# Row sums of the softmax: from a column of ones in the products to ScalarE's accumulator

## The chip, the cores and the metric

The kernel runs on one core of a Trainium2 chip. The metric is the device time of one execution in microseconds; the median of three runs before the change is 420.76 us (420.61 to 422.99). Everything is float32. The engines are TensorE (PE; its weight loads are PEld), VectorE (DVE), ScalarE (ACT), GpSimd (POOL) and SyncE (SP), which issues most DMAs. Each works through its own queue in order and waits on semaphores for the others.

## The reference

Cross-attention with a second, small set of image-prompt tokens. B = 8 batches, S = 112 queries, 20 heads of D = 16, 371 text tokens and NIP = 4 prompt tokens a batch:

```python
q = heads(hidden_states @ W_q)
k_t = heads(text_ehs @ W_k)
v_t = heads(text_ehs @ W_v)
probs_t = softmax(einsum('bhsd,bhtd->bhst', q, k_t) * attn_scale)
text_out = einsum('bhst,bhtd->bhsd', probs_t, v_t)
qsem = l2norm(einsum('bhst,bte->bhse', probs_t, text_ehs))
ip_n = l2norm(ip_ehs)
sem = einsum('bhse,bne->bhsn', qsem, ip_n)
fused = einsum('bhsd,bhnd->bhsn', q, k_ip) * attn_scale + 0.5 * sem
probs_ip = softmax(fused) * spatial_mask[None, None, :, None]
out = (text_out + einsum('bhsn,bhnd->bhsd', probs_ip, v_ip)) @ W_out + b_out + residual
```

The softmax over the 371 tokens divides by the row sum of its exponentials. The kernel keeps the exponentials undivided, multiplies them with everything that they meet, and divides once at the end; it therefore needs the row sum z of each query and head.

## The kernel before, in words

The work goes through 40 **steps**: for each of 8 batches b, five groups g of four heads (`steps`, line 1121). The four heads of a group sit on the four 32-row groups of TensorE and work side by side.

For one step, in the order of the data:

- `scores` (line 724) multiplies queries and keys of one head into a PSUM bank: 371 text columns and 4 prompt columns. The keys of all heads stand in `kT`, three pieces of T = 375 columns, one piece for every two groups.
- `probabilities` (line 753): VectorE takes the negated maximum of the row (line 757), ScalarE writes the exponentials to `p` (line 760) and copies the four prompt logits to `ipl` (line 762). `sent` (line 766) lets SP issue the DMA that carries `p` to the ring buffer `xg` in blocks of 28 queries, so that
- `turned` (line 771) can transpose them in 32x32 blocks on VectorE to `xgT`.
- `multiplied` (line 784) is the large product. Its stationary operand is a block of 32 tokens of the transposed exponentials of one head; its moving operand is a row of `u`. One head has 12 blocks. `u` holds, side by side, the Gram matrix of the batch's context (upper part only, so block j begins at column 32j), the products with the four normalised prompts, a column of ones, and the 16 values of the head. A product is therefore up to UW = 371 + 4 + 1 + 16 = 392 columns wide and ends 32 columns earlier with every block, 40 at the last one. A float32 product is two TensorE instructions in the trace.
- `value_sums` (line 807, ScalarE) copies the last 21 columns of the result to `pvs`: four prompt products, the row sum z (from the column of ones), and 16 value sums. `reduced` (line 839, VectorE) multiplies the first 371 columns with `p` again and sums them: that is the squared norm of `qsem`. In the last batch and at the end of the one before it, `shared` (line 812) does this for some heads on ScalarE and GpSimd, and ScalarE then sums with an accumulator output (line 836).
- `finish` (line 860) turns `pvs` and the norms of a whole batch into its output; z is read in lines 881 to 898. It runs in pieces, spread over the next batch. For the last batch it is split: 16 heads in `finish`, four in `last_heads` (line 1045).

`u` is built a batch ahead. The Gram matrix goes through PSUM to `ug` (ScalarE, line 512), whose constant columns are set once (lines 220 to 223), and from there by DMA into the four row groups of `u` (`gram_to_groups`, line 554). The values are put into the last 16 columns of each region by GpSimd (`placed`, line 696). The regions of a row begin at `GCOL` = 0, 392, 656, and a row quarter is `GW` = 792 columns.

The order on TensorE, SP, VectorE and, in the main loop, ScalarE is the order of the program text (`manual_schedule`); GpSimd is ordered by the framework until the last batch. The scores and exponentials run LEAD = 2 steps ahead of the products (`ahead`, line 1257): in step n, two scores of step n+2 are issued before the first block and two more after block j = 5, and in between the transposes for step n+1. After the blocks come `value_sums`, `reduced`, and then `between` (line 1132): one piece of the work for the next batch on TensorE (its Gram matrix, values, keys, queries) or of the output of the batch before. `pvs` and `u` have two buffers, used by the batches in turn; the products use four PSUM banks (`ps_qd`), each free again when both `value_sums` and `reduced` have read it.

Of the kernel before, what the change touches and what calls it, by code (L numbers as in the profile page):

```python
# [8 lines left out]
F32 = mybir.dt.float32  # L9
AF = mybir.ActivationFunctionType  # L10
ALU = mybir.AluOpType
# [3 lines left out]
NIP = 4  # L15
# [5 lines left out]
def kernel(  # L21
# [14 lines left out]
    nc = tc.nc  # L36
    P = 128
    B, S, C = x.shape
    T, E = ehs.shape[1:]
    H = HEADS  # L40
    D = C // H
    TT = T - NIP
# [7 lines left out]
    REST = C - FULL * P  # L50
    RG = 32
    HN = H * NIP
    VW = NIP + 1 + D
    UW = TT + VW
    UV = UW - D
    SCALE = D ** -0.5
# [8 lines left out]
    GCOL = [sum(WC[:c]) for c in range(NT + 1)]  # L65
# [7 lines left out]
    groups = [[i * HC + 2 * a + r for a in range(GROUP)] for i in range(2) for r in range(2)]  # L73
# [4 lines left out]
    work = ctx.enter_context(tc.tile_pool(name="work", bufs=2))  # L78
# [140 lines left out]

    ug = const.tile([P, GCOL[NT]], F32, tag="ug", name="ug")  # L220
    for c in range(NT):
        nc.gpsimd.memset(ug[:, GCOL[c + 1] - D - 1 : GCOL[c + 1] - D], 1.0)
        nc.gpsimd.memset(ug[:, GCOL[c + 1] - D : GCOL[c + 1]], 0.0)


# [178 lines left out]
    def begin(b):  # L404
        s = st[b] = dict(ct=loaded.pop(b))
        s["ctxT"] = work.tile([P, NE, TP], F32, tag="ctxT", name=f"ctxT_{b}")
        if b < LEAD:
            nc.gpsimd.memset(s["ctxT"][:, :, T:], 0.0)

        s["kT"] = work.tile([P, NC, T], F32, tag="kT", name=f"kT_{b}")  # L410
        s["k3"] = k3
        if b == 0:
            s["vd"] = dram.tile([TP, C], F32, tag="vd", name=f"vd_{b}", bufs=1)
        s["u"] = work.tile([P, UCOL], F32, tag="u", name=f"u_{b}")
        s["vr"] = work.tile([P, BLK, NG, D], F32, tag="vr", name=f"vr_{b}")
        s["ipl"] = work.tile([S, H, NIP], F32, tag="ipl", name=f"ipl_{b}")
        s["ss"] = work.tile([S, H], F32, tag="ss", name=f"ss_{b}")
        s["pvs"] = work.tile([S, H, VW], F32, tag="pvs", name=f"pvs_{b}")

    def dealt(b, c, t):  # L420

# [321 lines left out]
    def home(b, g):  # L743

        if b == B - 1 and g == 1:
            t = io.tile([P, NT, E], F32, tag="ct", name=f"p_{b}_{g}").rearrange("p c e -> p (c e)")
        elif b == B - 1 and g == 3:
            t = wv_sb.rearrange("p e f -> p (e f)")
        else:
            return work.tile([S, GROUP, TT], F32, tag="p", name=f"p_{b}_{g}", bufs=3)  # L750
        return t[:S, : GROUP * TT].rearrange("p (a t) -> p a t", t=TT)

    def probabilities(b, g, a, hold=False):
        s = st[b]
        ps = s.pop(("sc", g, a))
        nmx = small.tile([S, 1], F32, tag="nmx", name=f"nmx_{b}_{g}_{a}", bufs=4)
        nc.vector.tensor_reduce(nmx, ps[:S, :TT], AX.X, ALU.max, negate=True)  # L757
        if ("p", g) not in s:
            s["p", g] = home(b, g)
        nc.scalar.activation(s["p", g][:, a, :], ps[:S, :TT], AF.Exp, bias=nmx)  # L760
        if b > 0:
            nc.scalar.copy(s["ipl"][:, groups[g][a], :], ps[:S, TT:T])  # L762
        if not hold:
            sent(b, g, a)

    def sent(b, g, a):

        xg = x_ring[(b * NG + g) % NX]
        nc.sync.dma_start(xg[a * RG : a * RG + S // QN, :, :TT], st[b]["p", g][:, a, :])
# [37 lines left out]
    def value_sums(b, g, a0=0, a1=GROUP):  # L807
        s = st[b]
        for h, ps in list(zip(groups[g], s["qd", g]))[a0:a1]:
            nc.scalar.copy(s["pvs"][:, h, :], ps[:S, TT:UW])  # L810

    def shared(b, g, n):

        s = st[b]
        some = list(enumerate(zip(groups[g], s["qd", g])))[:n]
        if b == B - 1:
            t = work.tile([P, NE, TP], F32, tag="ctxT", name=f"shared_{b}_{g}")
            prods = [t[:S, a, :TT] for a, _ in some]
        else:

            t = work.tile([S, NIP, H, D], F32, tag="wv", name=f"shared_{b}_{g}", bufs=1)
            t = t.rearrange("p n h d -> p (n h d)")
            prods = [t[:, a * TP : a * TP + TT] for a, _ in some]
        p = s["p", g]
        for a, (h, ps) in some:
            if b == B - 1:
                nc.scalar.copy(s["pvs"][:, h, :], ps[:S, TT:UW])
            nc.scalar.copy(prods[a], ps[:S, :TT])
        yield

        for a, _ in some:
            nc.gpsimd.tensor_tensor(prods[a], prods[a], p[:, a, :], ALU.mult)
        yield

        for a, (h, _) in some:
            nc.scalar.activation(prods[a], prods[a], AF.Copy, accum_out=s["ss"][:, h : h + 1])
        yield
# [22 lines left out]
    def finish(b, heads=(0, H), bd=None):  # L860

        s = st[b]
        eng = nc.gpsimd
        h0, h1 = heads
        n = h1 - h0
# [11 lines left out]
        pvs = s["pvs"][:, part]  # L877
        if "xb" not in s:
            s["xb"] = work.tile([S, C], F32, tag="xb", name=f"xb_{b}", bufs=1)
            with_bias(b)  # L880
        z = pvs[:, :, NIP]

        z2 = sm("z2")
        nc.vector.scalar_tensor_tensor(z2, z, EPS * EPS, z, ALU.mult, ALU.mult)
# [2 lines left out]
        zr = sm("zr")  # L887
        attn = attn_ring[b % 2]
        ah = attn[:, :C].rearrange("p (h d) -> p h d", d=D)[:, part]

        def divided():
            eng.tensor_tensor(
                ah, pvs[:, :, NIP + 1 :], zr.unsqueeze(2).to_broadcast([S, n, D]), ALU.mult
            )

        if bd is not None:
# [33 lines left out]
        if bd is not None:  # L930
            ps = bank(f"ps_wT_{b}")
# [9 lines left out]
            ps = bank(f"ps_a_{b}_{h0}")  # L941
# [103 lines left out]
    def last_heads(b):  # L1045


        s = st[b]
        h0, n = FULL * HC, GROUP
        part = slice(h0, H)  # L1050

        def sm(name, *shape):
            return small.tile([S, n, *shape], F32, tag=f"{name}l", name=f"{name}_last", bufs=1)

        def over_ip(t):
            return t.unsqueeze(2).to_broadcast([S, n, NIP])

        pvs = s["pvs"][:, part]
        z = pvs[:, :, NIP]
        z2, rn, zr = sm("z2"), sm("rn"), sm("zr")  # L1060
        nc.vector.scalar_tensor_tensor(z2, z, EPS * EPS, z, ALU.mult, ALU.mult)
        yield

        nc.vector.tensor_tensor(rn, s["ss"][:, part], z2, ALU.max)
        nc.vector.reciprocal(zr, z)
        attn = attn_ring[b % 2]
        nc.vector.tensor_tensor(
            attn[:, :C].rearrange("p (h d) -> p h d", d=D)[:, part],
            pvs[:, :, NIP + 1 :],
            zr.unsqueeze(2).to_broadcast([S, n, D]),  # L1070
            ALU.mult,
        )
        nc.scalar.activation(rn, rn, AF.Sqrt)
        nc.scalar.preload_act_table(AF.Exp)
        ps = ps_qd.tile([P, 512], F32, tag="qd", name=f"ps_a_{b}_{h0}")
        nc.tensor.transpose(ps[:, :S], attn[:, FULL * P :], ident[:S, :S])
        yield

        nc.vector.reciprocal(rn, rn)
        fu, ex, w = sm("fu", NIP), sm("ex", NIP), sm("w", NIP)  # L1080
        nc.vector.tensor_tensor(fu, pvs[:, :, :NIP], over_ip(rn), ALU.mult)
        nc.vector.scalar_tensor_tensor(fu, fu, SEM_SCALE, s["ipl"][:, part], ALU.mult, ALU.add)
        mx, sx, rx = sm("mx"), sm("sx"), sm("rx")
        nc.vector.tensor_reduce(mx, fu, AX.X, ALU.max)
        nc.vector.tensor_tensor(fu, fu, over_ip(mx), ALU.subtract)
        nc.scalar.activation(ex, fu, AF.Exp)
        yield

        aT = work.tile([P, NC, S], F32, tag="aT", name=f"aT_{b}_{h0}")
        nc.scalar.copy(aT[:, FULL, :], ps[:, :S])  # L1090
        nc.vector.tensor_reduce(sx, ex, AX.X, ALU.add)
        nc.vector.reciprocal(rx, sx)
        nc.vector.scalar_tensor_tensor(w, ex, sm_sb, over_ip(rx), ALU.mult, ALU.mult)
        yield

        k = n * NIP
        ps = ps_qd.tile([P, 512], F32, tag="qd", name=f"ps_wT_{b}_{h0}")
        nc.tensor.transpose(ps[:k, :S], w.rearrange("s h n -> s (h n)"), ident[:S, :S])
        wT = small.tile([S, S], F32, tag="wTl", name="wT_last", bufs=1)
        nc.scalar.copy(wT[:k], ps[:k, :S])  # L1100
        yield

        nc.tensor.matmul(
            s["o"][:S, :C], aT[:, FULL, :], wo_sb[:, FULL, :], start=False, stop=False
        )
        nc.tensor.matmul(s["o"][:S, :C], wT[:k], s["bw"], start=False, stop=True)
        yield

        ob = work.tile([S, C], F32, tag="xb", name=f"ob_{b}", bufs=1)
        nc.vector.tensor_tensor(ob, s["o"][:S, :C], s["xb"], ALU.add)  # L1110
        nc.sync.dma_start(out[b], ob)
        del st[b]
        yield
# [247 lines left out]
    b = B - 1  # L1361
# [6 lines left out]
    for g in range(NG):  # L1368
# [7 lines left out]
        for j, _ in enumerate(multiplied(b, g)):  # L1376
# [8 lines left out]
            if g == 1 and j in (2, 3):  # L1385
                for a in ((3, 2), (1, 0))[j - 2]:
                    ps = ps_qd.tile([P, 512], F32, tag="qd", name=f"ps_s_{b}_{NG - 1}_{a}")
# [9 lines left out]
        n = (3, 3, 2, 1)[g]  # L1397
# [93 lines left out]
```

## Time and profile before

| | before |
|---|---|
| median of 3 runs | 420.76 us |
| the profiled execution's own time | 420.08 us |
| its span, first to last instruction | 418.3 us |
| TensorE busy | 410.9 us, 98% |
| VectorE busy | 334.5 us, 80% |
| ScalarE busy | 216.3 us, 52% |
| GpSimd busy | 123.6 us, 30% |
| the products of line 797, busy on TensorE | 218.5 us, 3840 instructions |
| the exponentials of line 760, busy on ScalarE | 84.5 us, 156 instructions, and 4 that write elsewhere |

A row of a group of instructions reads: line, engine, operation, output<-inputs by name, shape of output<-input, count, then busy time in us and the mean of one in ns, then idle time of the engine just before them and what ended it. A row of the timeline reads: start in us, length in us, engine, line, operation, names, shapes, count. A row of the chain reads: start, length, what. A row of the waits: who waited for whom, us in total, times, the longest. PE's matmuls overlap in the pipeline and the ends of their records are modelled, so starts say more than lengths. A wait for several semaphores is put down to the one that came last.

### The profile page before, as it was taken

The numbers are of one execution on the slowest core, as the hardware profiler recorded it, in microseconds if no ns is written. First come the engines' busy times: TensorE is split into PE (matmuls) and PEld (weight loads), VectorE is DVE, ScalarE is ACT, GpSimd is POOL, SyncE is SP. The second block draws the span as 40 slices with busy tenths as digits, with TensorE's granted clock in tenths as the row PEclk, the third lists the DMA queues.
The fourth block names the chain that finished last, engine by engine and source line by source line (L and its number), as shares of the span: only waits on it lengthen the run. The fifth ranks groups of instructions, "written<-read, shape, count | busy, mean of one in ns | idle before, by whom it ended". The sixth has DMA issues, their size and how long they took to land.

```text
span 418.3 us, 14151 instructions
## 1 busy us (share of the span) xinstructions
PE 410.9 (98%) x5512; PEld 321.4 (77%) x5512; DVE 334.5 (80%) x724; ACT 216.3 (52%) x732; POOL 123.6 (30%) x308
## 2 busy tenths in 40 slices
PE   8999999999999999999999999999999999989996
PEld 8767777787778877788777877788678887677983
DVE  4037689988899889898898978899798977878774
ACT  2344334736365453746356353654538463765774
POOL 3611121112071114422062121712144120724540
PEclk9999999999999999999999999999999999999999
DMA  8777856557764455465554555554445355526201
GB/s 247 211 189 201 184 144 155 150 133 172 176 164 130 134 142 142 113 157 164 142 134 126 170 133 136 133 126 143 121 123 137 97 169 151 144 75 168 69 2 31
DMA packets 47578, 58.98 MB, mean 141 GB/s; under 512 B 10648, under 2 KB 41536, under 8 KB 47510
## 3 DMA queue, kind: packets, MB, share of 16 engines
q1 hardware_dynamic: 46878, 57.10, 51.8%
q10 hardware_dynamic: 632, 0.96, 0.8%
q8 instruction: 44, 0.72, 0.8%
q14 instruction: 24, 0.20, 0.2%
HBM read 16.79 MB, written 1.88 MB: 45 GB/s over the span
## 4 chain that ended last, share of the span: by engine, by line
PE 90%; DVE 3%; POOL 2%; ACT 2%; DMA 2%; issue 1%; SPq 0%; DVEq 0%; POOLq 0%
PE ps_qd L797 37%; PE ps_v L616 13%; PE ps_s L734 10%; PE ps_k L582 10%; PE ps_g L540 7%; PE ps_q L381 3%; PE ps_o L1011 3%; PE ps_g L496 1%; DMA xg<-p 1%; DVE nmx L757 1%; ACT p L760 1%; DVE xgT L778 1%; PE ps_w L472 1%; PE ps_o L966 1%; PE ps_k L598 1%; POOL wv L986 1%
## 5 line engine op out<-in xcount | busy, mean ns | idle before, releaser
L797 PE MATMUL ps_qd<-u,xgT 32*112 32x168 f32 (+11 forms) x3840 | 218.5, 351 | 0.0
L797 PEld LDWEIGHTS ps_qd<-u,xgT 32*112 32x112 f32 x3840 | 185.0, 172 | 27.2 <-issue 0.7
L778 DVE STREAM_TRANSPOSE xgT<-xg 128x512 f32<-128x512 f32 (+2 forms) x79 | 126.0, 1604 | 4.3 <-DMA xg<-p 3.9
L760 ACT ACTIVATE p<-ps_s,nmx 112x371 f32<-112x371 f32 x156 | 84.5, 579 | 86.5 <-DVE nmx L757 81.2
L757 DVE TENSOR_REDUCE nmx<-ps_s 112x1 f32<-112x371 f32 x160 | 78.4, 534 | 25.1 <-PE ps_s L734 24.1
L843 DVE CUSTOM_DVE_ANT_0 junk<-ps_qd,p 112x371 f32<-112x371 f32 x146 | 79.2, 543 | 20.3 <-ACT pvs L810 3.3
L703 POOL COPY u<-vr 128x64 f32<-128x64 f32 x120 | 26.7, 240 | 138.4 <-PE ps_qd L797 106.5
L734 PE MATMUL ps_s<-kT,qm 32*112 32x375 f32 (+1 forms) x320 | 65.8, 496 | 0.0
L616 PE MATMUL ps_v<-wv_sb,ctxT 128*128 128x384 f32 (+1 forms) x192 | 63.0, 477 | 0.0
L616 PEld LDWEIGHTS ps_v<-wv_sb,ctxT 128*128 128x128 f32 x192 | 35.7, 190 | 20.9
L582 PE MATMUL ps_k<-ctxT,wk_sb 128*128 128x371 f32 x136 | 46.9, 488 | 0.2 <-DVE ctxT L463 0.2
L734 PEld LDWEIGHTS ps_s<-kT,qm 32*112 32x112 f32 x320 | 25.6, 171 | 12.7 <-issue 10.8
L582 PEld LDWEIGHTS ps_k<-ctxT,wk_sb 128*128 128x128 f32 x136 | 24.4, 189 | 14.0 <-issue 0.5
L651 ACT COPY vr<-vext 32x240 f32<-32x240 f32 x84 | 32.7, 389 | 1.3
L623 ACT COPY vext<-ps_v 128x384 f32<-128x384 f32 (+1 forms) x24 | 11.2, 466 | 42.2 <-PE ps_v L616 42.2
L540 PE MATMUL ps_g<-ctxT 128*32 128x375 f32 (+11 forms) x672 | 30.4, 333 | 0.0
L540 PEld LDWEIGHTS ps_g<-ctxT 128*32 128x32 f32 x672 | 27.7, 110 | 2.0
L390 DVE TENSOR_SCALAR qm<-ps_q,emask 128x224 f32<-128x224 f32 (+1 forms) x25 | 9.0, 394 | 18.1 <-PE ps_q L381 18.0
L762 ACT COPY ipl<-ps_s 112x4 f32<-112x4 f32 x140 | 23.0, 165 | 0.0
L986 POOL TENSOR_TENSOR wv<-vip,w 112x1280 f32<-112x1280 f32 x6 | 14.8, 2468 | 22.2 <-DVE w L926 22.2
L512 ACT ACTIVATE ug<-ps_g 128x375 f32<-128x375 f32 (+2 forms) x24 | 8.3, 375 | 24.7 <-PE ps_g L540 12.5
L442 DVE STREAM_TRANSPOSE ctxT<-ct 128x512 f32<-128x512 f32 x18 | 20.0, 1113 | 0.0
(177 smaller groups left out, 344.2 us busy)
## 6 DMA issues: line engine op xcount, KB each, us to landing
xg<-p SPq DMA_DIRECT2D x156, 162.3 KB
u<-ug SPq DMA_DIRECT2D x124, 99.0 KB
ct<-in_ctx_dram SPq DMA_DIRECT2D x24, 176.0 KB
vip<-vipd SPq DMA_DIRECT2D x6, 560.0 KB
out_dram<-ob SPq DMA_DIRECT2D x8, 140.0 KB
ct<-in_ctx_dram SPq DMA_DIRECT2D x4, 256.0 KB
x_sb<-in_x_dram SPq DMA_DIRECT2D x7, 140.0 KB
xr_sb<-in_x_dram SPq DMA_DIRECT2D x28, 35.0 KB
```

The costliest lines, as they stand in the source:

```text
L540: nc.tensor.matmul(ps[c][q * RG : (q + 1) * RG, j * RG - c * P : T - c * P], ctxT[:, e, j * RG : (j + 1) * RG], ctxT[:, e, j * RG : T], st ...
L582: nc.tensor.matmul(ps[:, :TT], wk_sb[:, e, i * P : (i + 1) * P], s["ctxT"][:, e, :TT], start=(e == 0), stop=(e == NE - 1),)
L616: nc.tensor.matmul(ps[:, :w], ctxT[:, e, c * P : (c + 1) * P], wv_sb[:, e, :w], start=(e == 0), stop=(e == NE - 1),)
L651: copy(s["vr"][a * RG : (a + 1) * RG, q::QN].rearrange("p c g d -> p c (g d)"), s["vext"][q * RG : (q + 1) * RG, :, a * w : (a + 1) * w],)
L703: nc.gpsimd.tensor_copy(v, dealt(b, c, s["vr"][:, c * QN : (c + 1) * QN, g, :]))
L734: nc.tensor.matmul(ps[:S, :w], qm[a * RG : (a + 1) * RG, i, r, j * S : (j + 1) * S], s["kT"][a * RG : (a + 1) * RG, i, :w], start=True, st ...
L757: nc.vector.tensor_reduce(nmx, ps[:S, :TT], AX.X, ALU.max, negate=True)
L760: nc.scalar.activation(s["p", g][:, a, :], ps[:S, :TT], AF.Exp, bias=nmx)
L762: nc.scalar.copy(s["ipl"][:, groups[g][a], :], ps[:S, TT:T])
L778: nc.vector.transpose(xT[:, j0:j1].rearrange("p j (k q) -> p q j k", q=QN), xg[:, :, j0 * RG : j1 * RG].rearrange("p q (j k) -> p q j k", ...
L797: nc.tensor.matmul(banks[a][:S, j * RG : UW], xT[a * RG : (a + 1) * RG, j, :S], region(b, c)[a * RG : (a + 1) * RG, q, j * RG - c * P :], ...
L843: nc.vector.tensor_tensor_reduce(out=junk, in0=ps[:S, :TT], in1=s["p", g][:, a, :], scale=1.0, scalar=0.0, op0=ALU.mult, op1=ALU.add, accu ...
```

## The change

The column of ones leaves `u`. The exponential's ACTIVATE gets an accumulator output instead, which writes the row sum of what it has just computed to the last column of `pvs`. `pvs` keeps its width of 21: four prompt products, 16 value sums, and the row sum at the end. The products are one column narrower (391 to 39), `GCOL` becomes 0, 391, 654 and `GW` 789, and the copies of `value_sums` have 20 columns. The place of z in `finish` and `last_heads` moves accordingly.

```diff
-    VW = NIP + 1 + D
+    VW = NIP + D
     UW = TT + VW
     UV = UW - D
...
     for c in range(NT):
-        nc.gpsimd.memset(ug[:, GCOL[c + 1] - D - 1 : GCOL[c + 1] - D], 1.0)
         nc.gpsimd.memset(ug[:, GCOL[c + 1] - D : GCOL[c + 1]], 0.0)
...
-        s["pvs"] = work.tile([S, H, VW], F32, tag="pvs", name=f"pvs_{b}")
+        s["pvs"] = work.tile([S, H, VW + 1], F32, tag="pvs", name=f"pvs_{b}")
...
-        nc.scalar.activation(s["p", g][:, a, :], ps[:S, :TT], AF.Exp, bias=nmx)
+        h = groups[g][a]
+        nc.scalar.activation(s["p", g][:, a, :], ps[:S, :TT], AF.Exp, bias=nmx, accum_out=s["pvs"][:, h, VW:])
         if b > 0:
-            nc.scalar.copy(s["ipl"][:, groups[g][a], :], ps[:S, TT:T])
+            nc.scalar.copy(s["ipl"][:, h, :], ps[:S, TT:T])
...
-            nc.scalar.copy(s["pvs"][:, h, :], ps[:S, TT:UW])
+            nc.scalar.copy(s["pvs"][:, h, :VW], ps[:S, TT:UW])
...
-                nc.scalar.copy(s["pvs"][:, h, :], ps[:S, TT:UW])
+                nc.scalar.copy(s["pvs"][:, h, :VW], ps[:S, TT:UW])
...
-        z = pvs[:, :, NIP]
+        z = pvs[:, :, VW]
...
-                ah, pvs[:, :, NIP + 1 :], zr.unsqueeze(2).to_broadcast([S, n, D]), ALU.mult
+                ah, pvs[:, :, NIP:VW], zr.unsqueeze(2).to_broadcast([S, n, D]), ALU.mult
...
-        z = pvs[:, :, NIP]
+        z = pvs[:, :, VW]
...
-            pvs[:, :, NIP + 1 :],
+            pvs[:, :, NIP:VW],
```

The last two pairs are `last_heads`, the two before them `finish`.

## The prediction

> **What bounds the kernel now.** I read the page first: busy shares, chain, costliest group.
>
> ```profile
> span 418.3 us, 14151 instructions
> ...
> PE 410.9 (98%) x5512; PEld 321.4 (77%) x5512; DVE 334.5 (80%) x724; ACT 216.3 (52%) x732; POOL 123.6 (30%) x308
> ...
> PE 90%; DVE 3%; POOL 2%; ACT 2%; DMA 2%; issue 1%; SPq 0%; DVEq 0%; POOLq 0%
> ...
> L797 PE MATMUL ps_qd<-u,xgT 32*112 32x168 f32 (+11 forms) x3840 | 218.5, 351 | 0.0
> ```
>
> TensorE works through 98% of the span, and 90% of the chain that ended last is its own; ScalarE is half idle. The products that lose a column (line 797) are half of TensorE's time. So a gain must come from fewer TensorE columns, and the added ScalarE work costs only where TensorE already waits, directly or through VectorE. The view of waits gives TensorE few of its own, and the longest ends on GpSimd:
>
> ```profile
> PE ps_a L999 <- POOL attn L994: 1.7, 1, 1.7
> ```
>
> GpSimd's work ahead of it starts from products of TensorE, so it moves with them, and nothing in it touches the change.
>
> **What a column is worth.** Groups with shapes kept apart (the last two figures before the bar: busy us, mean ns), then the chain in order of time (start, us, what):
>
> ```profile
> L797 PE MATMUL ps_qd<-u,xgT 32*112 32x264 f32 x320 | 46.6, 381 | 0.0
> L797 PE MATMUL ps_qd<-u,xgT 32*112 32x232 f32 x320 | 42.8, 354 | 0.0
> L797 PE MATMUL ps_qd<-u,xgT 32*112 32x72 f32 x320 | 16.7, 246 | 0.0
> L797 PE MATMUL ps_qd<-u,xgT 32*112 32x40 f32 x320 | 16.3, 248 | 0.0
> ```
>
> ```profile
> 206.71 1.40 PE ps_qd L797 x49
> 210.81 2.58 PE ps_v L616 x8
> ```
>
> 32 columns fewer are 27 ns less, so 0.84 ns a column. The eight matmuls of line 616 (384 columns) give the same rate back to back: 2.58/8/384 = 0.84 ns. At 72 and 40 columns the duration stands still, so there a floor rules. A step (one batch, one group of four heads) has 12 blocks of 392 to 40 columns; four heads run side by side on the four row groups, and each product is two instructions (3840 = 40 steps x 12 x 4 x 2). The last six blocks, 720 columns, would take 720 x 2 x 0.84 = 1.21 us by columns; they took 1.40, and the excess is what the floor adds to the last two. So ten blocks shrink: 10 x 2 x 0.84 = 17 ns a step, 40 steps: **-0.67 us**. If the floor gave way too, 12 blocks make -0.81; this is the other end, and I take -0.67.
>
> [...]
>
> **What the accumulator read costs.** The kernel already has ScalarE sums, in the last batches (line 836):
>
> ```profile
> L836 ACT ACTIVATION_READ_ACCUMULATOR shared<-shared 112x1 f32 x11 | 2.7, 244 | 0.0
> ```
>
> ```profile
> 398.27 0.52 ACT L836 ACTIVATE shared<-shared 112x371 f32<-112x371 f32 x1
> 398.68 0.19 ACT L836 ACTIVATION_READ_ACCUMULATOR shared<-shared 112x1 f32 x1
> 398.78 0.50 ACT L836 ACTIVATE shared<-shared 112x371 f32<-112x371 f32 x1
> ```
>
> A second instruction follows each exponential. Its record lasts 0.24 us on the mean, but it starts before the ACTIVATE's record ends, and the next instruction starts 0.10 us after it. In a full queue it delays what is behind it by 0.095 us; the far end is the whole 0.244. I take 0.095, which stands in the nearest rows. 160 exponentials make 15 us on an engine with 200 us idle. What it delays: the copy of the prompt logits (762), the next exponential, the copies of line 810, and the DMA xg<-p (769) with what is queued behind it on SP, u<-ug among it. Two exponentials stand in a row, so 0.19 us arrives at line 810, and VectorE's product-sum (843), which follows the first of those copies, starts as much later:
>
> ```profile
> 121.47 0.59 ACT L760 ACTIVATE p<-ps_s,nmx 112x371 f32<-112x371 f32 x1
> ...
> 121.93 0.17 ACT L762 COPY ipl<-ps_s 112x4 f32<-112x4 f32 x1
> 121.98 0.44 ACT L810 COPY pvs<-ps_qd 112x21 f32<-112x21 f32 x4
> ...
> 122.24 0.54 DVE L843 CUSTOM_DVE_ANT_0 junk<-ps_qd,p 112x371 f32<-112x371 f32 x1
> ...
> 124.80 0.08 DVE L843 DVE_READ_ACCUMULATOR2_ANT ss<- 112x1 f32 x1
> ...
> 125.00 0.48 PE L734 MATMUL ps_s<-kT,qm 32*112 32x375 f32 x2
> ```
>
> ```profile
> DVE junk L843 <- ACT pvs L810: 3.3, 6, 0.6
> ```
>
> ScalarE goes through these rows without a pause, and the waits name line 810 as what VectorE waits for there. The fourth product-sum frees the last of four banks at 124.88; the next step's first blocks of that head stand behind its scores at 125.00. Margin 0.12. This is a short step (g=3 of a batch whose next queries are ready); 0.19 less 0.12, plus the 0.02 by which TensorE comes earlier, loses 0.09. It is the first of three such steps (124.9, 221.9, 319.0); the last reads
>
> ```profile
> 318.92 0.08 DVE L843 DVE_READ_ACCUMULATOR2_ANT ss<- 112x1 f32 x1
> ...
> 319.12 0.48 PE L734 MATMUL ps_s<-kT,qm 32*112 32x375 f32 x2
> ```
>
> so 3 x 0.09 = **+0.27**. Where no margin is left:
>
> ```profile
> 327.25 0.08 DVE L843 DVE_READ_ACCUMULATOR2_ANT ss<- 112x1 f32 x1
> ...
> 327.27 0.48 PE L734 MATMUL ps_s<-kT,qm 32*112 32x375 f32 x2
> ```
>
> Here VectorE ends at 327.33, after TensorE wanted the bank: **+0.2**. The direct wait:
>
> ```profile
> 83.58 1.40 PE L381 MATMUL ps_q<-xT,wq_sb 128*128 128x224 f32 x6 [0.40 <-ACT ipl L720]
> ```
>
> Two exponentials are ahead of it on ScalarE: **+0.19**. Entering the last batch, four stand in a row, the last at 374.11 (0.38 us):
>
> ```profile
> 374.11 0.62 ACT L760 ACTIVATE p<-ps_s,nmx 112x371 f32<-112x371 f32 x1
> ...
> 374.89 0.95 ACT L828 COPY shared<-ps_qd 112x371 f32<-112x371 f32 x2
> ...
> 376.08 1.22 PE L797 MATMUL ps_qd<-u,xgT 32*112 32x392 f32 x10
> ...
> 376.21 0.08 DVE L843 DVE_READ_ACCUMULATOR2_ANT ss<- 112x1 f32 x1
> ```
>
> ScalarE frees its two banks at 375.84, VectorE its last at 376.29, against a first block at 376.08: between 0.14 and 0.38, taken as **+0.3**. The later DMAs of p meet VectorE waiting rarely:
>
> ```profile
> DVE xgT L778 <- DMA xg<-p: 3.9, 5, 1.4
> ```
>
> Five of 79 transposes waited, turning data for the next step; at most 5 x 0.19, taken as **+0.1**.
>
> **The end.** The row sum z no longer comes with the copy that closes a group:
>
> ```profile
> 404.21 0.19 ACT L836 ACTIVATION_READ_ACCUMULATOR shared<-shared 112x1 f32 x1
> ...
> 404.49 0.19 DVE L884 SCALAR_TENSOR_TENSOR z<-pvs 112x16 f32<-112x16 f32 x1 [1.08 <-ACT pvs L810]
> 404.72 0.17 DVE L886 TENSOR_TENSOR rn<-ss,z 112x16 f32<-112x16 f32 x1
> ```
>
> Line 884 can run in the 1.08 us in which VectorE waits for the copy; line 886 then waits for the read that ends at 404.40 and starts near 404.45, 0.27 earlier, on the chain that leads to the output. If the wait is kept for the whole tile, nothing is won; taken: **-0.2**.
>
> **Costed at nothing.** The memset of ones on GpSimd, one element less in 160 copies of line 810/827, and u<-ug DMAs of 3156 instead of 3168 bytes a row: none is near the chain. A new wait could come from the double buffer of pvs: the exponentials of batch b+1 now write it while batch b runs, so they need batch b-1's readers done:
>
> ```profile
> 206.65 0.24 DVE L910 TENSOR_TENSOR fu<-pvs,rn 112x80 f32<-112x80 f32 x1
> ```
>
> ```profile
> 215.13 0.57 ACT L760 ACTIVATE p<-ps_s,nmx 112x371 f32<-112x371 f32 x1 [1.23 <-DVE nmx L757]
> ```
>
> The last reader is done 8 us before the first writer, so it is free.
>
> **The sum**: -0.67 - 0.2 + 0.27 + 0.2 + 0.19 + 0.3 + 0.1 = +0.2 us. The profiled execution took 420.08 us (span 418.3 and 1.8 around it), so 420.3; the median of the runs stands 0.68 above it, so **420.9**. Gain and loss cancel.
>
> **Rivals.**
> - *The waits are covered* (0.22): VectorE makes up the 0.19 in its 20% idle time, or the copies of line 810 are not what releases line 843. Then -0.67 to -0.81 and the end's -0.27 remain: 419.7. For it, other steps have room: most of VectorE's waits are for scores and end well before the bank is wanted. Against it, the row of waits for line 810.
> - *The read is paid in full* (0.15), slower: 0.244 each, 0.49 a pair. It decides wherever the margin is under 0.49: 0.49 at 83.6, 3 x 0.39, 0.49 at 327, 0.9 at 376, 0.25 for the DMAs, together 3.3 less 0.87: 423.2. Against it stand the three rows of line 836.
> - *The width does not count* (0.10): 391 columns cost as much as 392. Then only the +1.06 and -0.2 stay: 421.6. The gram's odd widths speak against it:
>
> ```profile
> L540 PE MATMUL ps_g<-ctxT 128*32 128x375 f32 x56 | 18.9, 481 | 0.0
> L540 PE MATMUL ps_g<-ctxT 128*32 128x343 f32 x56 | 17.5, 455 | 0.0
> ```
>
> - *Odd offsets* (0.05), slower: blocks of u begin at 391, 654 and multiples of 789 floats instead of even numbers, read by TensorE, written by GpSimd and DMA. From 2% on the 218.5 us of line 797 (4.4 us) this alone is over 1%; 3% give 427. Against it:
>
> ```profile
> L734 PE MATMUL ps_s<-kT,qm x320: 470/473/565, 23.8 to 388.2; 32*112 32x375 f32 x140, 32*112 32x371 f32 x20
> ```
>
> Two fifths of these scores read kT from an odd column (375), and minimum and median do not part. The Trainium skill, "SBUF — State Buffer", section Operand start alignment, asks only for a multiple of the element size and says that its runs timed nothing; by it nothing is excluded.
> - *The exponentials wait for the buffer after all* (0.03): one wait a batch, up to the next short step, 422.
>
> **How the numbers follow.** The forecast has 0.45. The range goes from the covered case (419.6) to the read in full (423.2) and leaves out the odd offsets and part of the edges. Within 1% (4.2 us, about what a measurement tells from no change) lie all cases but one; with something for what I have not seen: faster 0.02, same 0.92, slower 0.06.
>
> **What the profile will show.** Line 797's forms one column narrower, 0.84 ns shorter, its busy time down by 0.6 to 0.8; 160 reads of the accumulator, the next ScalarE row 0.1 behind each; the copies of line 810 0.19 later after the step's scores; the wait at 83.6 grown to about 0.6; line 884 ahead of the last copy. Wrong would be: reads that hold ScalarE for 0.2 us, line 797 slower per column, or a new wait ahead of line 760.

## The result and the profile after

The changed kernel takes 422.72 us (median of 20 runs, 421.25 to 425.19), the kernel before, measured beside it, 421.21 us (20 runs, 420.08 to 422.99). The ratio is 1.0034, with a 95% interval of 1.0019 to 1.0049: 0.8 to 2.1 us slower. That is inside the predicted range and inside the 1% that I called no change, but the forecast was +0.2 us, and the interval leaves that out. What follows asks where the other 1.3 us come from.

The page of the changed kernel (engines, then a group with busy us, mean ns and idle time):

```profile
span 420.5 us, 14305 instructions
...
PE 412.8 (98%) x5512; PEld 324.3 (77%) x5512; DVE 336.9 (80%) x724; ACT 230.5 (55%) x892; POOL 122.9 (29%) x305
...
L760 ACT ACTIVATION_READ_ACCUMULATOR p<-ps_s,nmx 112x1 f32 x156 | 31.5, 202 | 0.0
```

ScalarE has 160 instructions more, and the kernel is still TensorE's: the same 5512 matmuls. The products' shapes, kept apart, are one column narrower, as planned:

```profile
L797 PE MATMUL ps_qd<-u,xgT 32*112 32x263 f32 x320 | 46.7, 379 | 0.0
L797 PE MATMUL ps_qd<-u,xgT 32*112 32x231 f32 x320 | 43.0, 353 | 0.0
...
L797 PE MATMUL ps_qd<-u,xgT 32*112 32x39 f32 x320 | 17.2, 248 | 0.0
```

The means fall by a nanosecond or two where the width counts and stand still at the floor. The busy sums do not fall, but they are a poor measure here, since the records overlap; the time from step to step is a better one. The waits (who for whom, total, times, longest):

```profile
DVE junk L843 <- ACT pvs L810: 8.0, 12, 1.0
...
PE ps_q L380 <- ACT ipl L719: 0.6, 1, 0.6
```

Before they were 3.3 us in 6 waits, and 0.4. In both rows the wait for ScalarE has grown; whether the second is the change's doing is taken up below.

**Where the 1.3 us of the profile are.** I number the steps 0 to 39 (5b + g) and let a step begin with its first product, the first row of the widest form of line 797. From the first product to the end the profiled execution of before takes 382.30 us (35.99 to 418.29), that of after 383.62 (36.88 to 420.50): +1.32. The remaining 0.89 us of the 2.2 between the spans lie ahead of the first product, in TensorE's first matmuls, which are the same in both kernels (kernel before, then after, timeline of TensorE):

```profile
4.92 0.65 PE L472 MATMUL ps_w<-ident 128*128 128x128 f32 x4
5.41 0.64 PE L455 MATMUL ps_c<-ident,ct 128*128 128x128 f32 x4
```

```profile
4.82 1.06 PE L471 MATMUL ps_w<-ident 128*128 128x128 f32 x4
5.67 1.06 PE L454 MATMUL ps_c<-ident,ct 128*128 128x128 f32 x4
```

Four matmuls take 1.06 us in place of 0.65, although the profile's column of the granted clock (PEclk) reads 1.00 in both. In all twelve profiles of this study the 128-column matmuls start 0.21 us apart up to some moment and 0.11 us apart from then on. That moment lies between 4.7 and 5.1 us in the kernel before, between 6.7 and 7.1 us in the changed one, and between 4.6 and 7.9 us in the twelve; the later it is, the later the first product begins, at 35.95 to 37.35 us. These matmuls are the same in all twelve, so I do not charge this to the change. By the Trainium skill, "TensorE: Matmul & The Clock Gate", section What's actually happening, the clock rises at the edge of a free-running window, so that the moment of the rise varies by plus or minus half a microsecond; the rows agree with matmuls that are first slow and then fast, and a spread of some 3 us is wider than that.

The table gives, in ns, how much longer than in the kernel before a step was, for the changed kernel and for the experiments told below (each from its own profiled execution; a plus is a loss):

| steps | after | reads only | columns only | even pitch | six reads | other six | both steps | last batch |
|---|---|---|---|---|---|---|---|---|
| 2 to 4 | +382 | +387 | -56 | +307 | +1125 | +2165 | +1903 | +1381 |
| 8 | +127 | +153 | -10 | +712 | -1 | +1 | +141 | 0 |
| 9 to 17, each | -9.8 | 0 | -9.7 | -15.8 | 0 | 0 | 0 | 0 |
| 18 | +246 | +222 | -8 | +233 | 0 | +62 | +246 | -1 |
| 19 to 27, each | -10.3 | 0 | -9.6 | -15.7 | 0 | 0 | 0 | 0 |
| 28 | +219 | +227 | -9 | +231 | 0 | +53 | +214 | +1 |
| 35 | +507 | +518 | -60 | +505 | +10 | -5 | +2 | +516 |
| 36 and 37 | +228 | +253 | +238 | +257 | +203 | +204 | +211 | +244 |
| after the last product's end | -182 | -9 | -200 | -173 | -53 | -46 | -49 | -51 |

Two rows need care. In steps 2 to 4 the runs differ by 2 us among themselves, and runs with no accumulator read in these steps have the largest values (the last four columns). Steps 36 and 37 are 0.2 us longer in every other profile than in that of before, with or without reads in them. The kernel before has one profile; where it alone stands apart, a difference to it is no evidence for a cause. The last row is the tail of the kernel, from the end of the last product to the end of the span; it is 0.05 us shorter in the four runs on the right too, which leave it as it was.

### The profile page after: what moved, and what is told of

Its sections match the earlier page's. It is cut to its first block, busy times and chain, and to the rows that moved or that the text cites. A ratio compares the mean times of both kernels' runs of the same rounds, so it can differ in the third digit from the quotient of the medians.

```text
span 420.5 us, 14305 instructions
## 1 busy us (share of the span) xinstructions
PE 412.8 (98%) x5512; PEld 324.3 (77%) x5512; DVE 336.9 (80%) x724; ACT 230.5 (55%) x892; POOL 122.9 (29%) x305
## 4 chain that ended last, share of the span: by engine, by line
PE 74%; POOL 2%; issue 1%; ACT 1%; DVE 0%; DMA 0%; POOLq 0%; DVEq 0%
PE ps_qd L797 35%; PE ps_v L615 11%; PE ps_s L733 9%; PE ps_k L581 6%; PE ps_g L539 6%; PE ps_o L1011 3%; PE ps_q L380 2%; PE ps_k L597 1%; POOL wv L986 1%; POOL bd L685 0%; PE ps_a L999 0%; POOL vr L650 0%; PE ps_k L572 0%; POOL wv L992 0%; ACT L1432 0%
## 5 line engine op out<-in xcount | busy, mean ns | idle before, releaser
L797 PE MATMUL ps_qd<-u,xgT 32*112 32x167 f32 (+11 forms) x3840 | 219.9, 350 | 0.0
L797 PEld LDWEIGHTS ps_qd<-u,xgT 32*112 32x112 f32 x3840 | 186.9, 171 | 26.7 <-issue 0.7
L760 ACT ACTIVATE p<-ps_s,nmx 112x371 f32<-112x371 f32 x156 | 89.9, 577 | 85.2 <-DVE nmx L756 73.7
L733 PE MATMUL ps_s<-kT,qm 32*112 32x375 f32 (+1 forms) x320 | 67.2, 497 | 0.0
L733 PEld LDWEIGHTS ps_s<-kT,qm 32*112 32x112 f32 x320 | 26.5, 170 | 12.3 <-issue 10.6
L760 ACT ACTIVATION_READ_ACCUMULATOR p<-ps_s,nmx 112x1 f32 x156 | 31.5, 202 | 0.0
```

What stands on the lines that cost most here:

```text
L733: nc.tensor.matmul(ps[:S, :w], qm[a * RG : (a + 1) * RG, i, r, j * S : (j + 1) * S], s["kT"][a * RG : (a + 1) * RG, i, :w], start=True, st ...
L797: nc.tensor.matmul(banks[a][:S, j * RG : UW], xT[a * RG : (a + 1) * RG, j, :S], region(b, c)[a * RG : (a + 1) * RG, q, j * RG - c * P :], ...
```

## The experiments

**Reads only.** The kernel before, columns of ones and all; the exponentials also get the accumulator output, and nobody uses it.

```diff
-        nc.scalar.activation(s["p", g][:, a, :], ps[:S, :TT], AF.Exp, bias=nmx)
+        h = groups[g][a]
+        nc.scalar.activation(s["p", g][:, a, :], ps[:S, :TT], AF.Exp, bias=nmx, accum_out=s["pvs"][:, h, VW:])
```

> The accumulator reads alone: the products keep their column of ones and all widths, and the exponentials write a row sum as well, which nothing uses. My theory (each read puts 0.093 us into ScalarE's queue, and TensorE pays only at the few step boundaries where ScalarE is backed up) expects the whole loss without the columns' gain: steps 3 to 5 together +0.33, the three short steps about +0.13, +0.23 and +0.21, the two places in the last batch +0.5 and +0.25, in all +1.6 to +1.9 us against before, no other step longer, and no shortening of the steps. Rival one (the loss of the changed kernel came from its odd widths and offsets, not from the reads): under +0.5. Rival two (every read is paid in full, 160 x 0.2 us of it on the path): over +5.

Measured: 422.91 us against 422.02, ratio 1.0034 (1.0010 to 1.0058). The undisturbed steps are unchanged to the nanosecond, so a read costs nothing where ScalarE has time; all losses sit in a few steps, and they are those of the changed kernel; from the first product to the end its profile is 1.82 us longer than that of before, within the 1.6 to 1.9 expected. The price of one read, in the changed kernel (timeline of ScalarE: start, length, what):

```profile
219.55 0.57 ACT L760 ACTIVATE p<-ps_s,nmx 112x371 f32<-112x371 f32 x1
220.02 0.19 ACT L760 ACTIVATION_READ_ACCUMULATOR p<-ps_s,nmx 112x1 f32 x1
220.11 0.15 ACT L762 COPY ipl<-ps_s 112x4 f32<-112x4 f32 x1
```

The copy that used to start 0.46 us after the exponential starts 0.56 after it. Two exponentials in a row start 0.51 us apart in the kernel before and 0.60 in this one (steps 8, 18 and 28), so each read delays the queue by 0.09, not by its 0.19.

**Columns only.** The narrow products of the change without accumulators; the row sums are left out, and a constant 1 stands in their place.

```diff
+    z_one = const.tile([S, H], F32, tag="z_one", name="z_one")
+    nc.gpsimd.memset(z_one, 1.0)
...
-        z = pvs[:, :, NIP]
+        z = z_one[:, part]
```

> The narrower products alone: no column of ones, and no accumulator; the row sums are left out and z is a constant of one, so the division by the sum does nothing. My theory expects the gain without the loss: 0.010 us a step as in the changed kernel, so -0.35 to -0.45, and -0.2 at the end because z no longer waits for the last copy: -0.6 us against before, and the row of line 884 ahead of the last copy of line 810. The prediction's own term would give -0.67 and -0.2, -0.9. Rival (odd widths or offsets cost): no gain or a loss, with steps longer than before.

Measured: 420.96 us, ratio 0.9972 (0.9951 to 0.9994). The losses of steps 8, 18, 28 and 35 are gone, the tail is 0.2 shorter, but a step gains 9.6 ns and not 17. (One step, 34, from 369.35 us on, was 1.68 us longer in this profile: the granted clock reads 0.50 from 370 to 373 us there and 1.00 from 374 us on. Nothing of it shows in the median.)

**Even pitch.** The changed kernel with one unused column at the end of each region of `u`, so that the regions begin at 0, 392 and 656 again while the products stay 391 wide.

```diff
-    WC = [UW - c * P for c in range(NT)]
+    WC = [UW + 1 - c * P for c in range(NT)]
```

> The changed kernel with the regions of u padded back to 392, 264 and 136 columns: the products are 391 to 39 columns wide but their operands begin at the same offsets as before the change. If the odd offsets are why a step shrinks by 0.010 us and not by the 0.017 of the prediction, undisturbed steps shrink by 0.017 against before and the whole is 0.25 us faster than the changed kernel (+1.1 us against before). If the offsets do nothing (my expectation), the steps and the boundaries are those of the changed kernel, +1.3 us against before.

Measured: 423.82 us, ratio 1.0043 (1.0018 to 1.0068), not to be told from the changed kernel by its median. But the steps are told apart. Nine undisturbed steps, 9 to 17, in the kernel before, the changed kernel and this one (timeline of TensorE, first and last start):

```profile
124.61 0.58 PE L797 MATMUL ps_qd<-u,xgT 32*112 32x392 f32 x2
...
213.33 0.58 PE L797 MATMUL ps_qd<-u,xgT 32*112 32x392 f32 x2
```

```profile
125.93 0.58 PE L797 MATMUL ps_qd<-u,xgT 32*112 32x391 f32 x2
...
214.56 0.58 PE L797 MATMUL ps_qd<-u,xgT 32*112 32x391 f32 x2
```

```profile
125.57 0.58 PE L797 MATMUL ps_qd<-u,xgT 32*112 32x391 f32 x2
...
214.14 0.58 PE L797 MATMUL ps_qd<-u,xgT 32*112 32x391 f32 x2
```

88.72, 88.63 and 88.57 us: the column is worth 9.8 ns a step with the odd starts and 15.8 with the even ones. My expectation, that the starts do nothing, was wrong by 6 ns a step, 0.24 us in the whole kernel. The 6 ns do not follow the odd starts one by one, though. From the mean start of a block's eight instructions to that of the next (19 undisturbed steps of each profile), the even pitch wins 1.6 to 1.9 ns at each of the first nine blocks. In the changed kernel block 1, which begins at an odd column of `u` (821), wins the same 1.7, and block 2, at an even one (1642), takes 1.7 ns longer than before the change. So the layout costs; what about it costs is open.

**Sums first.** The changed kernel, but with the product-sums (line 843) issued ahead of the copies of line 810 in the groups g = 3, to shorten the way on which I had put the loss of the short steps.

```diff
-        value_sums(b, g)
+        if g != 3:
+            value_sums(b, g)
...
+            value_sums(b, g)
```

The second place is after the regrouping of the values that follows `reduced`.

> The changed kernel with one order exchanged, in the steps of g=3 alone: the product-sums of VectorE (843) are issued ahead of ScalarE's copies (810) of the same banks, and ScalarE copies after its regrouping of the values. VectorE then has no wait behind the exponentials there. My theory expects the losses at the three short steps (+0.13, +0.25, +0.22) to go and nothing else to change: 0.5 to 0.6 us faster than the changed kernel, about +0.8 us against before. Rival (the short steps lose on the scores or on the DMAs of p, not on this copy): the three losses stay.

Measured: 423.83 us, ratio 1.0056 (1.0030 to 1.0081). The sums did start earlier, by 0.40 to 0.45 us in steps 18 and 28, and steps 18 and 28 still lost 0.226 and 0.232. The long steps 13 and 23 lost 0.19 each: ScalarE's last copy of line 810 now waits for VectorE, the copy of line 1003 behind it comes 0.58 us later in step 13, and the next scores wait for that. This was the first sign that the product-sums have nothing to do with the loss of the short steps.

**Some groups.** Even pitch, with the column of ones kept at the end of the region; accumulators only in 29 of 40 groups, those whose reads I held to be free, and products of 391 columns only there.

```diff
+    def summed(b, g):
+        return b < B - 1 and (b, g) not in ((0, 4), (1, 0), (1, 1), (2, 0), (4, 0), (6, 0))
+
+    def ends(b, g):
+        return UW if summed(b, g) else UW + 1
```

> Accumulators only where ScalarE has time, on operands at even offsets: the column of ones moves to the end of each region (pitch 392, 264, 136), a group with accumulators multiplies 391 columns and the others 392. Without accumulators are the last batch and the groups whose exponentials are issued at a step boundary that lost time: (b, g) = (0,4), (1,0), (1,1), (2,0), (4,0), (6,0); 29 groups have them. My theory expects -0.016 us in each of the 29 steps with 391 columns, 0 in the others, no longer step at the boundaries after steps 3, 4, 8, 18 and 28 nor in the last batch: -0.46 us from first product to end against before, -1.8 against the changed kernel. Rival (any read costs wherever it stands): the boundaries keep part of their losses.

Measured: 422.13 us against 421.86, ratio 0.9998 (0.9974 to 1.0023). The steps 8, 18, 28 gained 16, 7 and 6 ns in place of their losses, and step 35 lost 18 ns in place of 507. By steps this is what the change can be at its best: 29 x 16 ns, some 0.46 us of 420, which this measurement can't tell from nothing.

**Six reads.** The kernel before, with reads only on heads 0 and 1 of the groups (2,0), (4,0), (6,0). These are the exponentials that ScalarE takes after block 5 of the steps 8, 18 and 28, right ahead of the copies of line 810.

```diff
+        acc = dict(accum_out=s["pvs"][:, h, VW:]) if (b, g) in ((2, 0), (4, 0), (6, 0)) and a < 2 else {}
```

> The kernel before with six accumulator reads of 160: heads a = 0 and 1 of the groups (2,0), (4,0) and (6,0), whose exponentials ScalarE runs right ahead of the copies that close the three short steps; nothing uses the sums. My theory expects the three losses of the reads-only kernel by themselves: +0.15 after step 8, +0.22 after steps 18 and 28, +0.6 us in all, and no other step changed by more than 0.02. If the losses come of all the reads' delays added up over a batch, six reads show next to nothing.

Measured: 421.62 us in one run. Steps 8, 18, 28: -1, 0, 0 ns. The first product-sum of step 18 starts 6.19 us after the step's first product, in the kernel before 5.99 (timeline of the six reads, then of before):

```profile
214.78 0.58 PE L799 MATMUL ps_qd<-u,xgT 32*112 32x392 f32 x2
...
220.97 0.54 DVE L845 CUSTOM_DVE_ANT_0 junk<-ps_qd,p 112x371 f32<-112x371 f32 x1
...
223.12 0.58 PE L799 MATMUL ps_qd<-u,xgT 32*112 32x392 f32 x2
...
223.53 0.08 DVE L845 DVE_READ_ACCUMULATOR2_ANT ss<- 112x1 f32 x1
...
223.66 0.18 PEld L799 LDWEIGHTS ps_qd<-u,xgT 32*112 32x112 f32 x3
```

```profile
219.32 0.52 DVE L843 CUSTOM_DVE_ANT_0 junk<-ps_qd,p 112x371 f32<-112x371 f32 x1
...
221.86 0.08 DVE L843 DVE_READ_ACCUMULATOR2_ANT ss<- 112x1 f32 x1
...
222.07 0.49 PEld L797 LDWEIGHTS ps_qd<-u,xgT 32*112 32x112 f32 x5
```

So the product-sums did become 0.2 later, exactly as my forecast has it, and yet this step and the next one are as long as before, 8.34 and 8.63 us: the margin that I read as 0.12 is at least 0.2. My theory of the short steps fell here. The last rows show what I had misread. The fourth sum of step 18 ends 0.27 us after the first product of step 19 before, and 0.49 after it here; the weight load that waits for its bank moves from 0.40 to 0.55. But the first product of that head starts at 0.71 in both, behind scores that start at 0.39, and I had taken the start of these scores for the moment at which the bank is needed. The same stands in the changed kernel: the load at 0.54, the product at 0.71.

**Other six.** The same with heads 2 and 3 of these groups, the pair that ScalarE takes at the start of the steps. The banks of this pair's scores are taken over by the scores of heads 0 and 1 at block 5.

```diff
-        ... and a < 2 else {}
+        ... and a >= 2 else {}
```

> The kernel before with accumulator reads on six exponentials only: heads 2 and 3 of the groups (2,0), (4,0), (6,0), the pair that is taken at the start of the steps 8, 18 and 28; the columns of ones stay and the sums that the reads write are not used. The changed kernel loses 0.13, 0.25 and 0.22 us in these three steps; the run with the reads on heads 0 and 1, the pair taken at block 5, lost nothing there, although its product-sums did start later. New theory: the scores of heads 0 and 1 at block 5 take over the two score banks of heads 2 and 3, and wait on TensorE for ScalarE's copies of the prompt logits (line 762), which stand 0.19 later behind the two reads; so this run loses about 0.13 to 0.15 in step 8 and 0.2 to 0.25 in the steps 18 and 28, about 0.6 in all, and nothing in the other steps. Rival, my forecast's theory (product-sums behind the copies of line 810, which only the reads of heads 0 and 1 delay): nothing in any of the three steps. A third case: the loss needs the reads of both pairs; then this run too shows nothing, or less than half.

Measured: 423.47 us in one run (its steps 2 to 4 were 2.2 us longer), 422.23 before. Steps 8, 18, 28: +1, +62, +53 ns. Neither the old theory nor the new one: the third case, both pairs, or something with both.

What the trace of the changed kernel has that neither run of six has is a late *beginning*: the first exponential of step 18 starts 2.02 us after the first product, in the kernel before 1.80. VectorE computes its maxima later, because it comes later out of step 17, where its product-sums wait for the copies of line 810 behind the reads of that step. The start of step 18 in the kernel before, then in the changed kernel (timeline; L734 and L733 are the scores, PEld their weight loads):

```profile
213.33 0.58 PE L797 MATMUL ps_qd<-u,xgT 32*112 32x392 f32 x2
...
215.13 0.57 ACT L760 ACTIVATE p<-ps_s,nmx 112x371 f32<-112x371 f32 x1 [1.23 <-DVE nmx L757]
...
216.10 0.17 ACT L762 COPY ipl<-ps_s 112x4 f32<-112x4 f32 x1
...
216.58 0.47 PE L734 MATMUL ps_s<-kT,qm 32*112 32x375 f32 x1
...
221.67 0.58 PE L797 MATMUL ps_qd<-u,xgT 32*112 32x392 f32 x2
```

```profile
214.56 0.58 PE L797 MATMUL ps_qd<-u,xgT 32*112 32x391 f32 x2
...
216.58 0.57 ACT L760 ACTIVATE p<-ps_s,nmx 112x371 f32<-112x371 f32 x1 [1.45 <-DVE nmx L756]
...
217.74 0.17 ACT L762 COPY ipl<-ps_s 112x4 f32<-112x4 f32 x1
...
217.96 0.17 PEld L733 LDWEIGHTS ps_s<-kT,qm 32*112 32x112 f32 x1
...
218.11 0.47 PE L733 MATMUL ps_s<-kT,qm 32*112 32x375 f32 x1
...
223.15 0.58 PE L797 MATMUL ps_qd<-u,xgT 32*112 32x391 f32 x2
```

Counted from the step's first product, the second copy of the prompt logits starts at 2.77 before and 3.18 after, 0.41 later: 0.22 from the late beginning, 0.19 from two reads. It ends at 217.91, and 0.05 later the weights of the second score are loaded: TensorE stood there. Before, the copy ended at 216.27 and the scores followed at 216.58 with time to spare. The step takes 8.34 and 8.59 us.

**Both steps.** To test this, reads on heads 2 and 3 of (2,0), (4,0), (6,0), and on heads 0 and 1 of (1,4), (3,4), (5,4), which come in the step before.

```diff
+        acc = dict(accum_out=s["pvs"][:, h, VW:]) if (b, g, a < 2) in [(c, 0, False) for c in (2, 4, 6)] + [(c - 1, NG - 1, True) for c in (2, 4, 6)] else {}
```

> The kernel before with accumulator reads on twelve exponentials: heads 2 and 3 of (2,0), (4,0), (6,0), taken at the start of the steps 8, 18 and 28 (the run with these alone lost 0, 0.06 and 0.05 us there), and heads 0 and 1 of (1,4), (3,4), (5,4), taken at block 5 of the steps before, 7, 17 and 27, where the copies of line 810 follow them; the columns of ones stay and the sums are not used. Theory now: the reads of step 17 make its product-sums (line 843) about 0.16 late, VectorE carries this into step 18 to the maxima of heads 2 and 3, the two reads there add 0.19, so the second copy of the prompt logits of that pair ends 0.35 to 0.4 late, and of this TensorE's scores at block 5 lose what is above a margin of 0.16 (0.12 in step 8). So: 0.13 to 0.15 in step 8, 0.2 to 0.25 in the steps 18 and 28, as in the changed kernel, and nothing in the other steps. Rival: the reads of heads 0 and 1 within the steps 8, 18 and 28 are needed too, since ScalarE enters the step late or by a way that I have not seen; then about 0, 0.06 and 0.05, as with six reads.

Measured: 423.17 us in one run, 423.28 before. Steps 8, 18, 28: +141, +246, +214 ns, the losses of the changed kernel, from 12 reads of 160. Step 18 (timeline):

```profile
215.88 0.58 PE L799 MATMUL ps_qd<-u,xgT 32*112 32x392 f32 x2
...
219.06 0.17 ACT L764 COPY ipl<-ps_s 112x4 f32<-112x4 f32 x1
...
219.28 0.17 PEld L734 LDWEIGHTS ps_s<-kT,qm 32*112 32x112 f32 x1
...
224.47 0.58 PE L799 MATMUL ps_qd<-u,xgT 32*112 32x392 f32 x2
```

The copy starts at 3.18, the weight load follows its end (219.23) by 0.05, the step takes 8.59. In step 18 of these runs the loss is the lateness of this copy less 0.16: 0.41 gives 0.25 (changed kernel, both steps), 0.38 gives 0.22 (reads only), 0.225 gives 0.06 (other six), 0.155 gives 0.01 beside the neighbouring steps (some groups, which has the reads of step 17 but not those of step 18), 0 gives 0 (six reads). In step 8, where the margin is 0.12, the rule also gives the +712 ns of the even pitch: the first exponential starts there at 2.49 and not at 1.84, and the second copy 0.84 later than before. Why VectorE came so late into that one step was not traced. The cause of the three losses is settled.

**Last batch reads.** The kernel before, with reads only in the last batch.

```diff
+        acc = dict(accum_out=s["pvs"][:, h, VW:]) if b == B - 1 else {}
```

> The kernel before with accumulator reads in the last batch alone (20 of 160), the sums unused. My theory expects +0.52 between steps 35 and 36 and +0.27 between steps 37 and 38, where four to six exponentials stand in a row on ScalarE ahead of the copies that free the banks, up to 0.05 more around step 34, and every step before 33 unchanged: +0.8 us. If these losses are carried in from earlier reads, they stay away.

Measured: 422.5 us in one run. Step 35 +516, step 37 +269 ns, as in the changed kernel. The first of the two is a read's work: the runs without reads in this batch (six reads, other six, both steps) have +10, -5 and +2 there. The second is not shown to be: those three lose 0.20 to 0.21 in steps 36 and 37 together, this one 0.24.

**First pairs.** Reads on heads 0 and 1 of (7,1) and heads 2 and 3 of (7,4) only: the first two of the six exponentials ahead of step 35, and the first two of the four ahead of step 37.

```diff
+        acc = dict(accum_out=s["pvs"][:, h, VW:]) if (b, g) in ((B - 1, 1), (B - 1, 4)) and a in ((0, 1), (2, 3))[g == 4] else {}
```

> The kernel before with accumulator reads on four exponentials of the last batch only: heads 0 and 1 of group (7,1), the first two of the six ahead of the wait at 376, and heads 2 and 3 of group (7,4), the first two of the four near 390; the columns of ones stay and the sums are not used. The changed kernel loses 0.51 in step 35 and 0.26 in step 37. Theory: ScalarE goes from the first of the six to the copies of lines 810 and 828 without a pause (a copy of 1.59 us lies between, and it is just as late), so each of the six reads counts 0.093 and step 35 loses 0.51 less four reads, about 0.14 to 0.19; step 37 loses its 0.26 less two reads, about 0.08. Rival for step 35: only the four exponentials right ahead of the copies count, as in my forecast; then nothing here. Rival for step 37: the loss comes with the last two of the four alone; then nothing here, or with any of them, then 0.26.

Measured: 422.15 us in one run, 422.23 before. Step 35 lost 0.24: the rival, by which the first two don't count, is out, and two reads cost rather more than the 0.14 to 0.19 that I expected. Step 37 lost 0.22 and not 0.08; with step 36 (-0.04) that is 0.18, no more than in the runs without any read there. So this part of the run tells nothing, and neither did the expectation.

The wait at step 35 in the changed kernel (timeline of ScalarE, VectorE, TensorE):

```profile
376.76 0.21 ACT L762 COPY ipl<-ps_s 112x4 f32<-112x4 f32 x1
376.81 0.47 ACT L810 COPY pvs<-ps_qd 112x20 f32<-112x20 f32 x4
...
377.24 0.54 DVE L843 CUSTOM_DVE_ANT_0 junk<-ps_qd,p 112x371 f32<-112x371 f32 x1 [0.61 <-ACT pvs L810]
...
377.75 1.37 PE L797 MATMUL ps_qd<-u,xgT 32*112 32x391 f32 x9
...
378.40 0.08 DVE L843 DVE_READ_ACCUMULATOR2_ANT ss<- 112x1 f32 x1
```

VectorE is free and waits 0.61 us for ScalarE's copies; its last sum frees a bank at 378.48, 0.73 after the step's first product. Before these were 376.29 and 376.08, 0.21. The difference, 0.52, is the loss of the step.

## Why the prediction was right, and where its steps were wrong

The verdict, no change within 1%, held; the sum was short by 1.3 us of 420. That it held is in part luck of a wide bound: any change under 4 us would have done, and of the five losses that I had added up one came by another way, one did not come and two can't be told from the noise. Term by term, from the profile of after, with 10 ns a step added back for the narrower products where a step holds both:

- *Columns, -0.67.* About 10 ns a step, -0.4 in all. Ten of twelve blocks shrink at 0.84 ns an instruction, as I had it: the even pitch gives 15.8 ns of the 17. The missing 6 ns come with the layout of `u`, where my fourth rival (odd offsets) had looked for a cost, but they are 0.24 us in place of its 4.4. I had read from the scores that odd starts cost nothing; there a 6 ns effect spread over 96 instructions can't be seen.
- *The read, 0.095 each.* Held (0.09). The rival of the full 0.244 is out.
- *Three short steps, +0.27.* This step of the prediction failed. The loss came to +0.62, by another way: not the product-sums ahead of the next step's first blocks, but TensorE's scores at block 5, which wait for the banks of the first pair. I had counted the two reads ahead of one wait, and not that VectorE carries the lateness of one step into the next, so that four reads come together. The first copy of a pair's logits stood in no row that I had weighed.
- *At 327, +0.2.* Did not come: step 30 is 0.01 longer (0.07 with reads only). It is the same misreading as at the short steps: VectorE's last sum ends 0.57 us after the step's first product in the changed kernel and 0.40 before, with no loss. It was not tried by itself, and three of the five runs without reads in this step are 0.08 shorter there than the kernel before, so some hundredths can't be read at all.
- *The direct wait at 83.6, +0.19.* Not shown. The row of the waits went from 0.4 to 0.6, and its step (4) lost 0.16. But the six runs that have reads elsewhere and none in the steps 2 to 4 show 0.5 to 1.3 in this row and lose 0.13 to 1.13 in step 4.
- *Entering the last batch, +0.3.* The mechanism held; mis-sized. +0.52, since six reads stand ahead of the wait and not four: ScalarE's copy of 1.59 us between the first two and the rest leaves no gap that could take them up.
- *The DMAs of p, +0.1.* Steps 29 to 34 lost 0.13 in all; what of it is these DMAs was not told apart.
- *The end, -0.2.* -0.18 against the profile of before; the runs that leave the tail as it was have -0.01 to -0.05. VectorE computes z ahead of the last copy, and line 886 follows the read (timeline of VectorE and ScalarE, changed kernel):

```profile
405.72 0.48 DVE L884 SCALAR_TENSOR_TENSOR z<-pvs 112x16 f32<-112x16 f32 x1
...
406.62 0.19 ACT L836 ACTIVATION_READ_ACCUMULATOR shared<-shared 112x1 f32 x1
406.71 0.15 ACT L810 COPY pvs<-ps_qd 112x20 f32<-112x20 f32 x1
406.83 0.18 DVE L886 TENSOR_TENSOR rn<-ss,z 112x16 f32<-112x16 f32 x1 [0.63 <-ACT shared L836]
```

- *Costed at nothing.* The double buffer of `pvs` made no wait that the runs show: steps 5 to 7 and 9 to 17 of the reads-only kernel are as long as before.

What the runs show to be the change adds up to -0.4 + 0.62 + 0.52 - 0.18, some +0.6. The rest of the 1.32 is 0.41 in the steps 2 to 4, 0.25 in the steps 36 and 37, where the profiles differ as much without the change, and 0.13 in the steps 29 to 34 (each with its columns added back). How much of these 0.8 us is the change stays open; the medians, 1.5 us apart (0.8 to 2.1), ask for some of it and don't say which. That the kernel with reads in some groups only stands at 0.9998 (0.9974 to 1.0023), and the columns alone at 0.9972, does not contradict this: the change has some 0.6 us to win (0.4 by the columns, 0.2 at the end), and the reads in a few steps take more than that.

## What to carry to other kernels

An engine that is half idle still sets the pace at single moments: before adding work to it, look in every stage for the instruction whose result releases a PSUM bank, and count all the added instructions since that engine (and the one that feeds it) last stood idle, over the border of the step as well. A margin read from two rows is a guess until a run moves one of them: here two runs of six reads each refuted what the timeline seemed to say. And compare step by step with more than one profile of the reference, or the noise of its one execution is booked as a cause.

## What the runs showed of the hardware that was not expected

- **The layout of the moving operand** can cost 6 ns a step of 96 float32 instructions: 9.8 ns won with regions at 0, 391 and 654 and rows of 789 floats, 15.8 with 0, 392 and 656 and rows of 792, the products 391 columns wide in both. The Trainium skill, "SBUF — State Buffer", section Operand start alignment, allows any multiple of the element size and says that its runs timed nothing; these runs agree that it is allowed, and show that a layout with odd starts isn't quite free. Which of the two, starts or row length, makes the difference was not tried.
- **An accumulator read overlaps with the end of its exponential**: its record lasts 0.20 us on the mean, the queue loses 0.09.
- **The start of the kernel varies by itself**: the matmuls go from 0.21 to 0.11 us apart at a moment between 4.6 and 7.9 us, which the granted clock, 1.00 throughout, does not show; the first product comes at 35.95 to 37.35 us, and steps 2 to 4 vary by up to 2 us. In the run of both steps one transposition waited 2.7 us for its data between 57 and 87 us, in the kernel before 1.1 at most (waits of that stretch, run of both steps):

```profile
DVE xgT L780 <- DMA xg<-p: 3.3, 2, 2.7
```
